# Two of seven additions of exponentials carried out by accumulating transfers from GpSimd's queue

## The chip, the cores and the metric

The kernel runs on one core of one Trainium2 chip. The metric is the time of one execution on the device, in microseconds (us). Before the change three timed runs took 2121.02, 2121.77 and 2122.29 us; their median, 2121.77 us, is the time before. A profile of one further execution is what all readings of the kernel before rest on. TensorE is called PE below, VectorE DVE, ScalarE ACT, GpSimd POOL, and SyncE, which issues nearly all transfers, SP.

## What is computed

Sixteen independent batches of 1024 nodes with 256 channels pass two layers, all in float32. The first layer builds an adjacency weighted by the likeness of node means, makes queries from it, and attends with four heads of 64 channels; the second is two graph convolutions. Each ends in a residual and a layer norm. The part that the change touches is the softmax of the attention:

```
g = relu(einsum('bcn,bnm->bcm', fea, adj * A_s) * para)     # queries, from the weighted adjacency
k, v = split(x @ kv_w)
attn = softmax(einsum('bhnd,bhmd->bhnm', q, k) * scale, axis=-1)
out  = einsum('bhnm,bhmd->bhnd', attn, v)
x = layernorm(x + out)
h = relu(graph_conv(x, adj, w1)); h = relu(graph_conv(h, adj, w2))
x = layernorm(x + (x + h) * 0.5)
```

The softmax is taken without its maximum: the exponentials are summed, and the attention's output is divided by the sum afterwards.

## The kernel before, in words

**Tiles.** A *row tile* is a buffer of 128 partitions by 1024 floats (512 KB in all). There are 31 of them, under one tag, and nearly everything is kept in them: exponentials, sums, weighted adjacency, snapshots, loaded adjacency. A new row tile takes the buffer that has been free the longest by the program's order, and its first writer waits until the last user of that buffer is done. PSUM is cut into three *big* tiles of two banks each (tag `big`) and two tiles of one bank each (tag `bank`).

**Units.** The attention of a batch is done in four units: two pairs of heads (`pair` 0 and 1), and for each pair two halves of 512 queries (`j`). Units 0 and 1 are the first pair, 2 and 3 the second; units 0 and 2 are the first of their pairs. In one unit the 1024 keys are eight tiles of 128 (`mt`, 0 to 7). For each, PE writes the scores of two heads into PSUM (L703), ACT takes the exponential into a row tile `pr` (L710; for `mt` 2 and 6 in two halves from two single banks, L708), and DVE adds the row tiles into a sum `acc`: `pr` 0 plus `pr` 1 (L722), then `pr` 2 to 7 one after the other (L724), seven additions in a unit. Then `turned_sum` transposes the sum in blocks of 32 (L731) and `part_sum` reduces it (L737) to the part of the softmax's denominator.

**Order.** The order of all instructions on each engine is written out by hand: the program is emitted under a manual schedule, every engine and every issuing queue takes its instructions in that order, and one that waits holds up all behind it. The loop over batches overlaps three of them: the attention of batch b, the queries for b+1, the convolutions of b-1 and b-2. From batch 2 on the attention is emitted by `both_units(pair)` (L762): first the scores of the pair's first unit with its additions in between (`collect`, called from `scores` at L713, then `partial` at L715), then the scores of the second unit without additions, then the second unit's additions woven between other steps, the products with the values of the first unit (`outputs`, L749), DVE's transpose of that result out of a big PSUM tile (L774), the products of the second unit into a single bank, and DVE's transpose of that (L778). The single bank that L778 frees is one of the two that the next pair's scores need for the halves of their `mt` 2.

**After the two pairs** PE goes on with the inner product of the first convolution (L903), the joined convolutions (`Joined.run`, L1180 and the products of L1017), the queries of the next batch (L648) and its keys and values. DVE follows with weights (L566, L620 to L623), the division by the denominators (L793 to L799), the sum uT (L1220) with the differences of L1006 to L1008 that the products of L1017 read, and the norms.

**Queues.** SP's queue issues all loads and stores of the steady state, in program order. POOL computes a few sums of the convolution (L1171 to L1174), of the queries (L607 to L610) and the powers for the norms (L361, L316); before the change it issues no transfer.

Batches 0 and 1 have an order of their own; their attention is not touched by the change.

Of the kernel before, what the change touches and what calls it, by code (L numbers as in the profile page):

```python
# [13 lines left out]
ALU = mybir.AluOpType  # L14
# [4 lines left out]
def kernel(  # L19
# [31 lines left out]
    nc = tc.nc  # L51
# [3 lines left out]
    NT = N // P  # L55
# [5 lines left out]
    NJ = N // FB  # L61
# [37 lines left out]
    def row_tile(name):  # L99
        return work.tile([P, N], F32, tag="row", name=name, bufs=ROWS)  # L100
# [16 lines left out]
    for t0 in range(0, NT, 2):  # L117
        nc.sync.dma_start(out=x_first[:, t0:t0 + 2, :],
                          in_=x[0, t0 * P:(t0 + 2) * P, :].rearrange("(t p) c -> p t c", p=P))
# [157 lines left out]
    class NodeSums:  # L277


        def __init__(self, q, xb, name):  # L280
            self.q, self.name = q, name
            self.square = squares[len(taken) % 2]
            taken.append(name)
            q.c_col = self.square[:, 0:NT]
            for t in range(NT):
                nc.scalar.activation(xb[:, t, :], xb[:, t, :], AF.Identity, accum_out=self.square[:, t:t + 1])
# [388 lines left out]
    class Attention:  # L675
# [6 lines left out]
        def __init__(self, b, xB, qT, kT, v):  # L682
            self.b, self.xB, self.qT, self.kT, self.v = b, xB, qT, kT, v
            self.o, self.pr = {}, {}

            self.rden = small.tile([P, len(UNITS) * FB // S], F32, tag="rden", name=f"rden_{b}", bufs=2)
            self.sums = small.tile([P, NC, NB], F32, tag="sums", name=f"sums_{b}", bufs=2)
# [27 lines left out]
                self.partial(u)  # L715

        def collect(self, u, *mts):
            prs = self.pr[u]
            for mt in mts:
                if mt == 1:  # L720
                    self.acc = row_tile(f"acc_{self.b}_{u}")
                    nc.vector.tensor_add(self.acc, prs[0], prs[1])  # L722
                elif mt > 1:
                    nc.vector.tensor_add(self.acc, self.acc, prs[mt])  # L724

        def partial(self, u):
            self.part_sum(u, self.turned_sum(u))
# [863 lines left out]
```

## Time and profile before

The profiled execution took 2121.55 us by its own timing, of which 2119.8 us lie between its first and last instruction (the span). The three timed runs have their median 0.22 us above the profiled one.

| what | value |
|---|---|
| time before, median of 3 runs | 2121.77 us (2121.02 to 2122.29) |
| profiled execution, its own time | 2121.55 us |
| its span | 2119.8 us |
| PE busy | 2108.4 us (99%) |
| DVE busy | 1866.9 us (88%) |
| ACT busy | 1136.1 us (54%) |
| POOL busy | 335.1 us (16%) |
| granted PE clock | 0.999 |
| DMA, moved in all | 346.36 MB, 163 GB/s over the span |
| SP's queue, share of the 16 DMA engines' span | 62.4% |
| one batch in the steady state (start of the scores to the next start) | 130.31 us |

How to read the profile: a busy time is that of one engine, and the engines run beside each other, so that the sum of busy times is no time of the kernel. The page gives busy times by engine, then the chain of work that ended last, followed back from the last instruction, by engine and line, then groups of instructions of one line and form with their count, busy time and mean duration. The timeline lists one engine's instructions in order, merged where several of one line follow each other; in brackets stands the idle time before an instruction and what ended it. A window's row sums what each engine was busy between two times, and the share of the time in which the 16 DMA engines were busy; that share can exceed 1, since the packets of one engine overlap.

### The profile page before, as it was taken

To read this page: it belongs to the slowest core of one execution; us is meant where nothing else is said; L and a number is where in the kernel's file an instruction comes from. 1 tells how busy PE (TensorE), PEld (TensorE's weight loads), DVE (VectorE), ACT (ScalarE), POOL (GpSimd) and SP (SyncE) were. 2 spreads that over 40 slices of the span, in tenths; PEclk is the share of its full clock that TensorE was granted. 3 is DMA by queue.
4 is the path that set the end of the run, shared out by engine and by line. 5 is a ranking of instruction groups with operands and counts; after the bars stand their busy time and mean duration, and the time that the engine had idled before them with its cause. 6 is when DMAs were issued, how large, how long until landed. Compare 5 with 4: busy or idle time off the path is not lost.

```text
span 2119.8 us, 24940 instructions
## 1 busy us (share of the span) xinstructions
PE 2108.4 (99%) x8708; PEld 1031.8 (49%) x8708; DVE 1866.9 (88%) x2271; ACT 1136.1 (54%) x1669; POOL 335.1 (16%) x209
## 2 busy tenths in 40 slices
PE   9999999999999999999999999999999999999998
PEld 5344435445454454545545454454544535445354
DVE  6899998898898988888988889888898888898875
ACT  5745564545646465463654736447355474555523
POOL 2011102131021311203112031210312102131021
PEclk9999999999999999999999999999999999999999
DMA  9495664756639476384864748557495573956545
GB/s 214 121 180 188 131 185 144 153 181 135 204 110 198 175 133 224 104 171 175 142 217 117 160 173 168 196 123 171 150 178 186 142 178 125 191 177 132 176 131 176
DMA packets 613715, 346.36 MB, mean 163 GB/s; under 512 B 491984, under 2 KB 556880, under 8 KB 613584
## 3 DMA queue, kind: packets, MB, share of 16 engines
q1 hardware_dynamic: 613312, 344.45, 62.4%
q8 instruction: 70, 1.15, 0.2%
q14 instruction: 61, 0.50, 0.1%
q10 hardware_dynamic: 272, 0.26, 0.0%
HBM read 294.45 MB, written 50.20 MB: 163 GB/s over the span
## 4 chain that ended last, share of the span: by engine, by line
PE 96%; DVE 1%; SPq 1%; DMA 1%; ACT 0%; issue 0%; POOL 0%; POOLq 0%; DVEq 0%; ACTq 0%
PE s L703 20%; PE av L749 20%; PE hu_ps L1180 17%; PE g_ps L648 16%; PE v_ps L448 4%; PE k_ps L444 4%; PE hu_ps L1017 4%; PE t_ps L903 3%; PE hu_ps L910 2%; PE g_ps L574 1%; PE h_ps L925 1%; PE u_ps L954 1%; PE h_ps L1017 1%; DVE acc L724 1%; SPq L108 1%; SPq L229 0%
## 5 line engine op out<-in xcount | busy, mean ns | idle before, releaser
L724 DVE TENSOR_TENSOR acc<-acc,pr 128x1024 f32<-128x1024 f32 x384 | 481.1, 1253 | 35.0 <-ACT pr L710 0.5
L710 ACT ACTIVATE pr<-s 128x1024 f32<-128x1024 f32 x392 | 391.6, 1120 | 173.0 <-PE s L703 172.7
L703 PE MATMUL s<-qT,kT 64*128 64x512 f32 x2048 | 449.8, 593 | 0.9 <-ACT qT L581 0.6
L749 PE MATMUL av<-pr,v 128*64 128x512 f32 x2048 | 447.0, 594 | 0.0
L703 PEld LDWEIGHTS s<-qT,kT 64*128 64x128 f32 x2048 | 196.5, 187 | 242.6 <-issue 182.2
L749 PEld LDWEIGHTS av<-pr,v 128*64 128x64 f32 x2048 | 144.0, 137 | 297.3 <-issue 270.3
L1180 PE MATMUL hu_ps<-adj,R 128*128 128x512 f32 x480 | 213.6, 592 | 0.0
L361 POOL TENSOR_TENSOR rstd<-rstd,neg_half 128x32 f32<-128x32 f32 x16 | 88.3, 5521 | 624.8 <-DVE rstd L359 624.8
L1171 POOL TENSOR_TENSOR R<-h 128x512 f32<-128x512 f32 x14 | 29.4, 2101 | 811.3 <-DVE o L774 648.7
L566 DVE SCALAR_TENSOR_TENSOR wg<-wg,adj 128x1024 f32<-128x1024 f32 x128 | 150.1, 1211 | 3.6 <-ACT wg L561 3.6
L708 ACT ACTIVATE pr<-s 128x512 f32<-128x512 f32 x240 | 143.1, 708 | 0.7 <-PE s L703 0.7
L560 ACT ACTIVATE wg<-c_row,c_sums 128x1024 f32<-128x1024 f32 x120 | 139.7, 1164 | 2.4 <-DVE wg L566 0.9
L1180 PEld LDWEIGHTS hu_ps<-adj,R 128*128 128x128 f32 x480 | 89.0, 190 | 100.9 <-issue 100.7
L561 ACT ACTIVATE wg<-wg 128x1024 f32<-128x1024 f32 x128 | 135.4, 1057 | 4.1
L906 ACT COPY t<-t_ps 128x1024 f32<-128x1024 f32 x16 | 16.2, 1014 | 175.1 <-PE t_ps L903 175.1
L648 PE MATMUL g_ps<-wg,x 128*128 128x512 f32 x224 | 107.7, 593 | 0.0
L648 PE MATMUL g_ps<-T,xB 128*128 128x512 f32 x208 | 107.3, 597 | 0.0
L648 PE MATMUL g_ps<-wg,xB 128*128 128x512 f32 x208 | 106.2, 592 | 0.0
L1180 PE MATMUL hu_ps<-adj,t 128*128 128x512 f32 x240 | 105.7, 592 | 0.0
L722 DVE TENSOR_TENSOR acc<-pr,pr 128x1024 f32<-128x1024 f32 x64 | 77.8, 1216 | 21.2 <-ACT pr L710 21.1
L731 DVE STREAM_TRANSPOSE accB<-acc 128x1024 f32<-128x1024 f32 x64 | 79.7, 1245 | 2.2
L737 DVE TENSOR_REDUCE den_part<-accB 128x32 f32<-128x1024 f32 x64 | 76.8, 1201 | 1.2
(251 smaller groups left out, 3062.6 us busy)
## 6 DMA issues: line engine op xcount, KB each, us to landing
adj<-adjT SPq DMA_DIRECT2D x210, 512.0 KB
adj<-in_adj_dram SPq DMA_DIRECT2D x128, 512.0 KB
para<-in_L_gnn_para_dram SPq DMA_DIRECT2D x32, 512.0 KB
xB_a<-in_x_dram SPq DMA_DIRECT2D x128, 128.0 KB
x1d<-xB_a SPq DMA_DIRECT2D x128, 128.0 KB
x<-x1d SPq DMA_DIRECT2D x16, 1024.0 KB
xB<-in_x_dram SPq DMA_DIRECT2D x120, 128.0 KB
x<-in_x_dram SPq DMA_DIRECT2D x15, 1024.0 KB
```

Source lines behind the costliest of these rows:

```text
L361: nc.gpsimd.tensor_tensor(self.rstd, self.rstd, neg_half, ALU.pow)
L560: nc.scalar.activation(wg, self.c_row, AF.Abs, bias=self.c_col[:, t:t + 1], scale=-1.0)
L561: nc.scalar.activation(wg, wg, AF.Tanh, scale=-0.5 / C)
L566: nc.vector.scalar_tensor_tensor(wg, wg, 1.0, self.adj.pop(t), op0=ALU.add, op1=ALU.mult)
L648: nc.tensor.matmul(self.p[n], x_n[:, k, :], w_n, start=(k == 0), stop=(k == TJ - 1))
L703: nc.tensor.matmul(halves[s], self.kT[rows, pair, ts(mt, P)], self.qT[rows, pair, ts(j, FB)], start=True, stop=True)
L708: nc.scalar.activation(pr[:, ts(s, FB)], halves[s], AF.Exp)
L710: nc.scalar.activation(pr, ps, AF.Exp)
L724: nc.vector.tensor_add(self.acc, self.acc, prs[mt])
L749: nc.tensor.matmul(pav[s * HD:(s + 1) * HD, :], self.v[:, mt, pair * P + s * HD:pair * P + (s + 1) * HD], prs[mt][:, ts(s, FB)], start=(mt ...
L1017: nc.tensor.matmul(dst[:, ts(t, P)], a[:, ts(t, P)], w, start=first, stop=True, skip_group_check=not first)
L1180: nc.tensor.matmul(dst, self.x[n][:, k, :], of_rows(rows, k), start=(start and k == 0), stop=(k == TJ - 1), skip_group_check=again)
```

## The change

From batch 2 on (14 of 16 batches), the first unit of each pair sums its exponentials in another way. `pr` 0 and 1 are added by DVE into an additional row tile (`acc2`). `pr` 2 and `pr` 3 are added into that tile by two transfers issued from POOL's queue, with addition at the destination. DVE adds `pr` 4 and 5 into `acc`, then `pr` 6 and 7, and last `acc2`. DVE so makes five additions in such a unit and not seven; POOL issues two transfers of 512 KB. There are 28 such units, so 56 transfers. The second unit of a pair and batches 0 and 1 stay as they were.

```diff
         def __init__(self, b, xB, qT, kT, v):
             self.b, self.xB, self.qT, self.kT, self.v = b, xB, qT, kT, v
             self.o, self.pr = {}, {}
+            self.aside = b >= 2
...
         def collect(self, u, *mts):
+            if self.aside and u % NJ == 0:
+                self.collect_aside(u, *mts)
+                return
             prs = self.pr[u]
...
+        def collect_aside(self, u, *mts):
+            prs = self.pr[u]
+            for mt in mts:
+                if mt == 1:
+                    self.aside_acc = row_tile(f"acc2_{self.b}_{u}")
+                    nc.vector.tensor_add(self.aside_acc, prs[0], prs[1])
+                elif mt in (2, 3):
+                    nc.gpsimd.dma_start(out=self.aside_acc, in_=prs[mt], accum_op=ALU.add)
+                elif mt == 5:
+                    self.acc = row_tile(f"acc_{self.b}_{u}")
+                    nc.vector.tensor_add(self.acc, prs[4], prs[5])
+                elif mt > 5:
+                    nc.vector.tensor_add(self.acc, self.acc, prs[mt])
+                if mt == NT - 1:
+                    nc.vector.tensor_add(self.acc, self.acc, self.aside_acc)
```

In the program as built, the second of the two transfers waits on POOL for the first to have landed, since both add into the same tile, and DVE's last addition waits for the second. The additional row tile also moves the buffers of some later row tiles by one place; among them is the first adjacency tile that SP loads for the next batch in the second pair: before, it took the buffer of `accB` of unit 1, and after, that of `acc2` of unit 2.

## The prediction

> **What bounds the kernel now.** I read the page's busy times and chain first, then who waited for whom, then the timeline of one steady batch (913.96 to 1044.27 us; the next starts 130.31 us later).
>
> ```profile
> PE 2108.4 (99%) x8708; PEld 1031.8 (49%) x8708; DVE 1866.9 (88%) x2271; ACT 1136.1 (54%) x1669; POOL 335.1 (16%) x209
> ...
> PE 96%; DVE 1%; SPq 1%; DMA 1%; ACT 0%; issue 0%; POOL 0%; POOLq 0%; DVEq 0%; ACTq 0%
> ```
>
> PE is busy all but 11.4 of 2119.8 us, and the chain that ended last is PE to 96%. The waits of PE itself say the same:
>
> ```profile
> PE idle L1253 <- POOL ident masks.py:199: 1.5, 1, 1.5
> PE good_ps L1534 <- DVE x L1100: 1.0, 1, 1.0
> PE s L703 <- ACT qT L581: 0.6, 1, 0.6
> PE s L703 <- DVE o L778: 0.3, 1, 0.3
> ```
>
> Over the whole run PE waited 1.3 us for DVE. So nothing that DVE saves can shorten the run by more than about that; work taken from DVE is worth nothing unless it comes to stand on PE's path. What DVE can do is be late. The last line names the place: L778 frees the PSUM bank that the next pair's scores need. How late DVE may be is read from its timeline; batch 7, first pair:
>
> ```profile
> 917.11 1.21 DVE L722 TENSOR_TENSOR acc<-pr,pr 128x1024 f32<-128x1024 f32 x1
> 918.43 7.87 DVE L724 TENSOR_TENSOR acc<-acc,pr 128x1024 f32<-128x1024 f32 x6
> 926.33 1.25 DVE L731 STREAM_TRANSPOSE accB<-acc 128x1024 f32<-128x1024 f32 x1
> ...
> 933.23 0.21 DVE L290 STREAM_TRANSPOSE c_turned<-c_sums 128x32 f32<-128x32 f32 x1 [0.60 <-ACT x L286]
> ...
> 941.83 0.72 DVE L778 STREAM_TRANSPOSE o<-av 128x512 f32<-128x512 f32 x1 [1.75 <-PE av L749]
> ```
>
> Between unit 0's sum (done 926.33) and L778 DVE has 0.60 + 1.75 us of idle time. L778 ended at 942.55. PE began the next scores at 941.71 and makes 64 records in 13.93 us, 0.218 each; `mt` 0 and 1 are 8 records, the first half of `mt` 2 another 2, so the second half, which takes L778's bank, begins at 941.71 + 2.18 = 943.89, 1.34 us after L778. Slack of the first pair: 0.60 + 1.75 + 1.34 = 3.7 us. Batches 5, 10 and 14 show the same 0.60 and 1.75.
>
> Second pair: the sum is done at 954.09 (start of L731). Idle behind it: 1.38 us before the L778 at 969.64, then none until uT (L1220, done 996.69). PE reads uT in the products of L1017 some 999.3 (24 records of the third group begin at 1001.12, the two groups before take 0.89 each): 2.65 us later. Slack 1.38 + 2.65 = 4.0 us.
>
> **What the skill says.** "DMA: Bandwidth & Descriptors", *Anatomy of one DMA*: a transfer from GpSimd's queue costs about 2.0 us fixed plus its bytes over 436 GB/s; 512 KB is then 3.2 us, as an estimate. No transfer of that queue is in the trace before, but SP's packets of 4096 bytes took 159 ns at the median, and 8 of them per engine are 1.27 us, which agrees with the 1.20 us of the second term. The same page, *Rules for kernel authors*: an accumulating DMA reads its destination and writes it later, so another access must wait for its semaphore; this is why the second waits for the first. *Queues, rings and completion order*: each DMA engine takes turns between queues packet by packet; no run here shows it yet. "SBUF — State Buffer", *Who interferes with whom*: a DVE addition of two SBUF tiles contends with GpSimd's reads. The trace agrees: L724 took 3.40 us for two at 963.58, beside a POOL addition, against 2.44 for two elsewhere.
>
> **The change part by part.**
>
> *Removed:* two of seven DVE additions in 28 units: 56 x 1.25 us (L724's mean of 1253 ns) = 70 us of DVE's 1866.9. On PE's path: nothing. Even on DVE little comes early: `pr` 5 is only there at 920.74 (ACT's L710), so `pr` 4+5, 6, 7 run from 920.8 at 1.31 us each to 924.7, and the last addition could end at 926.0, 0.3 us before the 926.33 of now.
>
> *Added:* two transfers in a row, and DVE's wait. The first is issued when L722 is done and `pr` 2 is there, 918.4. If one takes T from its issue until the next instruction may go, the last addition starts at the later of 924.7 and 918.4 + 2T and ends 1.3 later. DVE's lateness against now is 918.4 + 2T + 1.3 - 926.33 = 2T - 6.6. Behind the waiting addition on DVE stand L731, L737, the second unit's additions, L774 and L778; who waits for these is PE at the bank. Second pair, same shape: issue 946.1 (L722 at 944.85 plus 1.23), lateness 946.1 + 2T + 1.3 - 954.09 = 2T - 6.7.
>
> *T.* The accumulate reads source and destination, so I double the data term: 2.0 + 2.4 = 4.4 us on idle DMA engines (estimate from the page). Low end 3.2 us, if the second read overlaps. High end about 9, if each packet waits behind a longer turn of SP's. The load differs by pair:
>
> ```profile
> 918.40:925.00 6.60, 6.60 (x34) 2.99 (x32) 6.12 (x5) 6.60 (x10) 0.00 (x0) 1.00 1.04 126
> ...
> 949.00:957.00 8.00, 8.00 (x40) 3.21 (x38) 7.62 (x7) 8.00 (x13) 0.00 (x0) 1.00 0.00 0
> ```
>
> The last two columns are the DMA share and GB/s: in the first pair SP's short packets fill the engines (1.04), in the second they are idle. An even share of the engines doubles the data term once more, 2.0 + 4.8 = 6.8; with turns by packet the long packets get more than half. First pair: between 4.4 and 6.8, I take 6.1. Second pair: 4.5.
>
> *Sum.* First pair: lateness 2 x 6.1 - 6.6 = 5.6, less the 3.7 of slack: PE waits 1.9 us. Second: 2 x 4.5 - 6.7 = 2.3, within its 4.0: nothing. A stall of PE shifts everything behind it alike, so it is not given back: 14 x 1.9 = 27 us. Against the profiled execution's own time 2121.55 + 27 = 2148.2; the median lies 0.2 above that: 2148.
>
> *Costed at nothing, with the cover.* POOL: after the two issues it has nothing until L1171 at 963.68, and L1172 waits until 974.56 anyway; a second pair of transfers later than that would delay the convolution. SP: the first adjacency load of the next batch (943.67) now waits for the last addition of unit 2, to about 957; the load behind it already waits for unit 2's L737 and goes at 956.61, and the reader is L566 at 971.38, so 10 us cover it. SP's own transfers lose 29 MB worth of engine time beside 346, in stretches whose loads are read 15 us or more later. ACT: its `wg` tile takes the buffer of `acc` of unit 2, so L560 at 957.55 may wait some 2 us; ACT then idles 9 us before L906. Descriptor writing may slow a DVE addition by up to 1 us: inside T's range.
>
> **Rivals.**
>
> *Hidden after all* (26%). If 2T stays under 10.3 in the first pair (T about 5.1) the slack takes all, and the time is that of before, 2121.8. For it: 4.4 us is the page's own price, and SP's packets there are 128 bytes, so they yield fast. Against it: both transfers lie wholly in stretches with shares of 1.04 to 0.88.
>
> *The turns are long* (20%). If a turn of SP's is many of its short packets, or the addition itself is slow, T is some 9 in the first pair and 6.5 in the second: lateness 11.4 and 6.3, waits of 7.7 and 2.3, 14 x 10 = 140 us: 2262. For it: 475,616 packets of 128 bytes in SP's queue. Against it: they take 13 ns each.
>
> *Faster* (2%): needs PE idle time to give back; the ends of the run hold at most the 1.3 us above, under a tenth of a per cent. That the change moves no work is excluded: DVE makes two additions fewer in each unit as built.
>
> **The numbers.** Forecast 52% (T of 5.2 to 7.5 in the first pair; 2123 to 2190), hidden 26%, long turns 20%, faster 2%. A measurement tells about 0.2%, 4 us, from no change. Faster 0.02, same 0.26, slower 0.72. The range takes in the hidden case and half of the long turns: 2120 to 2215.
>
> **What would show it.** DVE's busy time falls to about 1797 us. DVE's last addition has an idle time before it of about 6 us in the first pair and 2.5 in the second, put down to the transfer. PE's L703 waits for L778 about 1.9 us per batch, 27 in all, and for nothing else new; the batch takes 132.2 us. I am wrong if PE waits elsewhere (L1017 for uT, L648 for weights), if the second pair waits as long as the first, or if the batch stays at 130.31.

## The result, and the profile after

The changed kernel takes 2202.24 us (median of 4 runs, 2196.49 to 2206.62) against 2121.72 us before (4 runs, 2121.02 to 2122.29): a ratio of 1.038, 95% interval 1.035 to 1.041. That is 80 us slower, where the forecast was 27. The profiled execution is the shortest of the four, 2196.49 us with a span of 2194.7 us, 74.9 us above the span before; the granted PE clock is 0.990 where it was 0.999.

From the page of the kernel after, the busy times, three groups (the last two columns are busy time and mean, then the idle time before and who ended it), and the issue line of the new transfers (median us from issue to landing last):

```profile
PE 2137.8 (97%) x8708; PEld 1050.8 (48%) x8708; DVE 1784.5 (81%) x2215; ACT 1140.9 (52%) x1669; POOL 385.5 (18%) x265
...
L704 PE MATMUL s<-qT,kT 64*128 64x512 f32 x2048 | 478.6, 610 | 45.6 <-DVE o L798 45.6
...
L744 DVE TENSOR_TENSOR acc<-acc,acc 128x1024 f32<-128x1024 f32 x28 | 34.3, 1225 | 157.0 <-DMA acc<-pr 157.0
...
acc<-pr POOLq DMA_DIRECT2D x56, 512.0 KB, 5.3
```

DVE does 56 instructions less, 82 us of work, and it waits 157 us for the transfers. PE, whose instructions are the same 8708, is busy 29 us longer than before, and waits 46 us more. Its waits name the place (L798 is the L778 of before, L704 the L703; the lines behind the new function have moved by 20):

```profile
PE s L704 <- DVE o L798: 45.6, 14, 10.8
PE idle L1273 <- POOL ident masks.py:199: 1.5, 1, 1.5
PE good_ps L1554 <- DVE x L1120: 1.0, 1, 1.0
```

Fourteen waits, one in each of batches 2 to 15, all where the prediction put them: the scores of the second pair wait for the bank that DVE's last copy out of the first pair frees. The second pair makes none. Batch 7 on DVE, first pair (start, duration, what; in brackets the idle time before it):

```profile
952.37 1.22 DVE L735 TENSOR_TENSOR acc<-pr,pr 128x1024 f32<-128x1024 f32 x1
...
957.35 2.56 DVE L742 TENSOR_TENSOR acc<-acc,pr 128x1024 f32<-128x1024 f32 x2
968.31 1.23 DVE L744 TENSOR_TENSOR acc<-acc,acc 128x1024 f32<-128x1024 f32 x1 [8.40 <-DMA acc<-pr]
969.57 1.25 DVE L751 STREAM_TRANSPOSE accB<-acc 128x1024 f32<-128x1024 f32 x1
...
982.58 0.67 DVE L798 STREAM_TRANSPOSE o<-av 128x512 f32<-128x512 f32 x1
```

and on POOL, both pairs:

```profile
954.12 0.92 POOL L737 DMA_DIRECT2D acc<-pr  x1 [14.31 <-DVE acc L735]
961.36 0.86 POOL L737 DMA_DIRECT2D acc<-pr  x1 [6.33 <-DMA acc<-pr]
986.30 0.86 POOL L737 DMA_DIRECT2D acc<-pr  x1 [24.08 <-ACT pr L709]
991.99 0.86 POOL L737 DMA_DIRECT2D acc<-pr  x1 [4.82 <-ACT pr L711]
```

PE begins batch 7 35.25 us later than before, because of the batches ahead, and DVE's first addition moves with it (917.11 before). The sum's transpose begins at 969.57, where 926.33 + 35.25 = 961.58 would be on time: DVE is 8.0 us late. The two transfers take 954.12 to 968.31, 14.2 us or 7.1 each. Over the 14 batches this stretch has a mean of 13.6 us (11.9 to 16.6); in the second pair it is about 10.2.

**Where the 74.9 us are.** Three terms, read on PE in batches 7 and 9, second pair:

```profile
976.96 2.84 PE L704 MATMUL s<-qT,kT 64*128 64x512 f32 x10
983.30 13.94 PE L704 MATMUL s<-qT,kT 64*128 64x512 f32 x54 [3.50 <-DVE o L798]
...
1248.99 2.84 PE L704 MATMUL s<-qT,kT 64*128 64x512 f32 x10
1253.50 12.28 PE L704 MATMUL s<-qT,kT 64*128 64x512 f32 x54 [1.67 <-DVE o L798]
```

Undisturbed, the 64 records show as one line of 14.00 us. Batch 9 takes 1248.99 to 1265.78, 16.79 us; less its idle time of 1.67 that is 15.12, still 1.12 more than 14.00. The products of the two halves normally run side by side (their records start at the same moment); those on either side of the wait run alone, so that ten records take 2.84 us and not 10 x 0.218 = 2.18, and the drain of the last one, which shows as busy, stands open too. That is 1.12 us for each wait, whatever its length. The Trainium skill, "TensorE: Matmul & The Clock Gate", *Part 3: Packing small matmuls — row/col tiling*, says that products in distinct row groups of the array run concurrently; the trace agrees, and shows what it costs when one has to come alone.

Batch 7 takes 20.28 us: less 3.50 of idle time and the 15.12 there remain 1.66. The windows of the two, from the first product behind the wait (columns: stretch, length, busy PE, PEld, DVE, ACT, POOL with records, granted clock, DMA share, GB/s), say what it is:

```profile
983.30:986.70 3.40, 3.40 (x8) 1.52 (x10) 2.18 (x2) 0.60 (x1) 0.40 (x1) 0.50 1.02 380
1253.50:1256.90 3.40, 3.40 (x16) 1.66 (x18) 2.18 (x2) 1.98 (x3) 0.68 (x1) 1.00 1.02 387
```

Behind the wait of batch 7 the granted clock is half for 3.4 us, and 8 records of PE fall into it where batch 9 has 16. Eight of the 14 waits are followed by such a stretch: seven of 3.41 us, each costing about 1.7, and one of 13.65 us in batch 2. The same page, *Part 1: The HAM clock gate (the "warmup" mystery)*, says that the clock falls to 4/8 after an idle window of 3413 ns, counted by windows that run freely. The 0.50 and the 3.41 us agree; but here a wait of 2.3 us was enough in batch 4 and one of 3.1 was not in batch 12, so it is not a whole idle window that decides.

The traces show more when time is cut by these windows. All lowered stretches of this run begin whole multiples of 3.413 us from each other, to within 0.003 us. Continued to either side, this grid gives two windows for batch 4 (its wait is over at 576.05) and two for batch 12 (over at 1653.89):

```profile
573.66:577.07 3.41, 1.13 (x7) 0.55 (x8) 3.38 (x5) 0.88 (x2) 0.00 (x0) 1.00 0.96 293
577.07:580.48 3.41, 3.41 (x12) 1.39 (x10) 1.16 (x2) 1.62 (x2) 0.86 (x1) 0.50 1.02 392
...
1648.87:1652.28 3.41, 1.88 (x8) 0.57 (x4) 3.34 (x5) 2.43 (x3) 0.00 (x0) 1.00 0.72 179
1652.28:1655.69 3.41, 1.80 (x8) 0.88 (x10) 3.41 (x4) 0.60 (x1) 0.00 (x0) 1.00 0.98 384
```

The shorter wait lies within one window, which PE so spends idle for 2.28 us, and the next window is at half clock. The longer one is split, 1.53 and 1.61 us, and no window is lowered. In batches 2 to 15 of this run and of a1, c2, d1, d2 and d3 below, every full-clock window with 2.07 us or more of idle PE was followed by half clock, and none with up to 1.96 us was. In other runs less was enough: 1.93 us in d4 (between other products), 1.85 us in b2 and 1.44 in b3, so that about 2 us is no fixed limit.

One wait is 10.8 us, in batch 2. Here is batch 2 before, and the same line after:

```profile
288.72 2.84 PE L703 MATMUL s<-qT,kT 64*128 64x512 f32 x10
291.88 12.28 PE L703 MATMUL s<-qT,kT 64*128 64x512 f32 x54 [0.32 <-DVE o L778]
```

```profile
302.03 14.94 PE L704 MATMUL s<-qT,kT 64*128 64x512 f32 x54 [10.77 <-DVE o L798]
```

This is the wait of 0.3 us that the prediction quoted from before: in batch 2 DVE was already the late one, so its slack there was nothing, and the whole of the new lateness shows.

The sum: 45.6 - 0.3 of idle time, 13 x 1.12 = 14.6 for the waits that are new, 14.5 of lower clock (7 x 1.70, 2.66 in batch 2) = 74.4 of the 74.9 us. The 29 us that PE is busy longer are the last two of these terms.

### The profile page after: what moved, and what is told of

It is laid out like the page before. It is cut to its first block, busy times and chain, and to the rows that moved or that the text cites. A ratio compares the mean times of both kernels' runs of the same rounds, so it can differ in the third digit from the quotient of the medians.

```text
span 2194.7 us, 25011 instructions
## 1 busy us (share of the span) xinstructions
PE 2137.8 (97%) x8708; PEld 1050.8 (48%) x8708; DVE 1784.5 (81%) x2215; ACT 1140.9 (52%) x1669; POOL 385.5 (18%) x265
## 5 line engine op out<-in xcount | busy, mean ns | idle before, releaser
L704 PE MATMUL s<-qT,kT 64*128 64x512 f32 x2048 | 478.6, 610 | 45.6 <-DVE o L798 45.6
L704 PEld LDWEIGHTS s<-qT,kT 64*128 64x128 f32 x2048 | 214.8, 192 | 297.8 <-issue 189.1
L728 DVE TENSOR_TENSOR acc<-acc,pr 128x1024 f32<-128x1024 f32 x216 | 273.2, 1265 | 16.8 <-ACT pr L711 0.5
L737 POOL DMA_DIRECT2D acc<-pr x56 | 49.2, 878 | 672.4 <-DVE acc L735 347.1
L744 DVE TENSOR_TENSOR acc<-acc,acc 128x1024 f32<-128x1024 f32 x28 | 34.3, 1225 | 157.0 <-DMA acc<-pr 157.0
L740 DVE TENSOR_TENSOR acc<-pr,pr 128x1024 f32<-128x1024 f32 x28 | 34.3, 1225 | 84.0 <-ACT pr L711 84.0
```

The costliest lines, as they stand in the source:

```text
L704: nc.tensor.matmul(halves[s], self.kT[rows, pair, ts(mt, P)], self.qT[rows, pair, ts(j, FB)], start=True, stop=True)
```

## The experiments

Theory: all of the loss is the first pair's DVE lateness above its slack, with what a wait of PE brings along. Rivals: the second pair has a share; the transfers slow others by their traffic; the additional tile and its buffers do it.

**One pair only.** The condition `u % NJ == 0` becomes:

```diff
-            if self.aside and u % NJ == 0:
+            if self.aside and u == 0:      # a1_first_pair
+            if self.aside and u == NJ:     # a2_second_pair
```

> The transfers only in the first pair of each batch (unit 0), the second pair as before the change. Theory (two transfers in a row end too late for DVE's last addition, which holds up the transpose that frees PE's bank; only the first pair has too little slack): nearly the whole loss stays, 2190 to 2207 us, with some 45 us of PE waiting for L798. Rival (the cost is the 56 transfers' traffic, or comes from both pairs alike): half of the loss, near 2160 us.

> The transfers only in the second pair (unit 2), the first pair as before the change. Theory: the second pair's lateness of about 4 us is within its slack of 4.0, so 2121 to 2127 us and no wait of PE for DVE. Rival (both pairs alike): near 2160 us.

First pair alone: 2200.89 us, ratio 1.038 (1.036 to 1.040). Second pair alone: 2124.81, ratio 1.0016 (1.0009 to 1.0023). The waits of PE, first of a1, then of a2:

```profile
PE s L704 <- DVE o L798: 45.6, 14, 11.1
```

```profile
PE hu_ps L1037 <- DVE uT L1240: 3.2, 5, 0.6
```

The first pair is the whole loss. The second stands at the edge of its slack: five waits at the product that the prediction had named (L1017 of before), 3 us in all. In a2 the sum of unit 2 is 3.2 to 5.8 us late, and the five batches that wait are those with more than 4.4. With both pairs changed even these waits are absent: there PE itself comes out of the second pair's scores later, by 6.28 us in batch 7, and against that DVE is at most 3.8 us late in any batch.

**Traffic without the wait; the wait's removal without traffic.** In a3 DVE makes all seven additions, and the same 56 transfers go into a tile that nobody reads. In a4 DVE makes the five additions and no transfer is issued, so that exponentials 2 and 3 are missing from the sums.

```diff
             if self.aside and u % NJ == 0:
                 self.collect_aside(u, *mts)
-                return
...
-                    nc.vector.tensor_add(self.aside_acc, prs[0], prs[1])
+                    nc.gpsimd.memset(self.aside_acc, 0.0)
...
-                elif mt == 5:
...
-                if mt == NT - 1:
-                    nc.vector.tensor_add(self.acc, self.acc, self.aside_acc)
```

```diff
-                elif mt in (2, 3):
-                    nc.gpsimd.dma_start(out=self.aside_acc, in_=prs[mt], accum_op=ALU.add)
```

> DVE makes all seven additions as before the change; the same 56 transfers are issued at the same places, but add into a tile that POOL has filled with zeros and that nobody reads. Only the traffic, the issuing and the additional row tile are left. Theory (the wait is the cost): 2121 to 2125 us. Rival (traffic, descriptor writing or moved buffers cost): 2140 us or more.

> The five additions of the changed kernel without the transfers, so exponentials 2 and 3 are missing from the sums of the first units from batch 2 on. Theory: PE is the bound and 70 us less on DVE bring nothing, 2120.5 to 2122.5 us. Rival (DVE held PE somewhere that the waits do not show): some us faster, below 2117 us.

a3: 2122.31 us, ratio 1.0005 (0.9996 to 1.0014). a4: 2119.94, ratio 0.9994 (0.9985 to 1.0003), half a microsecond below the range I had expected. The traffic, POOL's issues and the tile cost nothing that can be told from noise (0.14% at most by the interval), and DVE's additions in a3 are not slowed by the issuing beside them (1867.2 us busy, before 1866.9). DVE's saving brings at most the 1.3 us by which a4 lies under the median of before, in which the wait of batch 2 is gone. What is left as the cost is that DVE waits.

**The wait moved behind other work.** b1 issues the same transfers, but the last addition of the first unit stands behind all of the second unit's additions, where the transfers have landed. With it go the transpose and the reduction of that sum, and the second unit's own transpose stands behind the copy that frees the bank, which takes 1.25 us of work from in front of the copy.

```diff
-            if summed:
+            if summed and not (self.aside and u % NJ == 0):
                 self.partial(u)
...
-                if mt == NT - 1:
-                    nc.vector.tensor_add(self.acc, self.acc, self.aside_acc)
...
+            first_acc, aside_acc = self.acc, self.aside_acc
...
-            accB = self.turned_sum(u + 1)
+            second_acc = self.acc
+            nc.vector.tensor_add(first_acc, first_acc, aside_acc)
+            self.acc = first_acc
+            self.partial(u)
...
-            self.part_sum(u + 1, accB)
+            self.acc = second_acc
+            self.partial(u + 1)
```

> All 56 transfers and five additions as in the changed kernel, but the first unit's last addition, its transpose and its reduction stand on DVE behind the second unit's additions, and the second unit's transpose and reduction behind L798's transpose. Theory (what costs is the place of the wait, ahead of the transpose that frees the bank): the transfers have landed by then, no wait of PE, 2121 to 2125 us. Rival (the chain of two transfers costs wherever its result is taken): 2140 us or more.

Measured 2121.78, ratio 1.0002 (0.9993 to 1.001): the loss is gone with all 56 transfers in place. DVE in batch 7; the last addition shows no idle time before it, as in 27 of the 28 units (1.4 us in the other):

```profile
938.17 1.22 DVE L796 TENSOR_TENSOR acc<-acc,acc 128x1024 f32<-128x1024 f32 x1
...
941.84 0.70 DVE L800 STREAM_TRANSPOSE o<-av 128x512 f32<-128x512 f32 x1
```

The copy that frees the bank starts at 941.84, as in the kernel before (941.83). DVE's busy share is 84%, 4 points below before, and the time is the same: PE bounds.

**Shorter chains of transfers.** b2 gives the two transfers a tile each (2 into 0+1, 5 into 3+4), so that they need not follow each other. b3 makes one transfer and six DVE additions.

```diff
-                elif mt in (2, 3):
-                    nc.gpsimd.dma_start(out=self.aside_acc, in_=prs[mt], accum_op=ALU.add)
+                elif mt == 2:
+                    nc.gpsimd.dma_start(out=self.aside_acc, in_=prs[2], accum_op=ALU.add)
+                elif mt == 4:
+                    self.aside_acc2 = row_tile(f"acc3_{self.b}_{u}")
+                    nc.vector.tensor_add(self.aside_acc2, prs[3], prs[4])
...
+                    nc.gpsimd.dma_start(out=self.aside_acc2, in_=prs[5], accum_op=ALU.add)
...
+                    nc.vector.tensor_add(self.acc, prs[6], prs[7])
                     nc.vector.tensor_add(self.acc, self.acc, self.aside_acc)
+                    nc.vector.tensor_add(self.acc, self.acc, self.aside_acc2)
```

```diff
-                elif mt in (2, 3):
+                elif mt == 2:
...
-                elif mt == 5:
+                elif mt == 4:
...
-                    nc.vector.tensor_add(self.acc, prs[4], prs[5])
+                    nc.vector.tensor_add(self.acc, prs[3], prs[4])
-                elif mt > 5:
+                elif mt > 4:
```

> Two transfers and five additions per first unit, but into two tiles: exponential 2 into the sum of 0 and 1, exponential 5 into the sum of 3 and 4; neither waits for the other. Theory (two landings in a row make the 14 us of the first pair): the second lands some 11 us after the first is issued and not 14, lateness near 3.5 us against a slack of 3.7, so 2121 to 2135 us, with waits left in the first batches. Rival (one loaded transfer alone is too slow): 2160 us or more.

> Only exponential 2 is added by a transfer; DVE makes six additions. Theory: one transfer of about 7 us lands when DVE reaches its last addition, lateness under 1.5 us in most batches, 2121 to 2124 us. Rival (one loaded transfer alone is too slow): 2150 us or more.

b3: 2123.49, ratio 1.0009 (1.0003 to 1.0016), with one wait, 1.4 us, in batch 2. b2: 2156.96, ratio 1.017 (1.015 to 1.019), between what the theory (2121 to 2135) and the rival (2160 or more) had led me to expect. Its waits:

```profile
PE s L704 <- DVE o L801: 15.1, 11, 5.8
```

In batch 7 its second transfer is issued 2.8 us after the first (938.52 and 935.76), because it needs DVE's addition of 3 and 4, and lands some 7.5 us later beside SP's loads: DVE is 4.2 us late there, beyond the slack. From the first issue to DVE's last addition these two take 10.4 us, where two in a row took 14.2: shorter, not half.

**Is it the clock?** b4 and c1 repeat the product ahead of the waiting one, to keep PE at work while it waits (5 and 3 times in place of one).

```diff
-                    nc.tensor.matmul(halves[s], self.kT[rows, pair, ts(mt, P)], self.qT[rows, pair, ts(j, FB)],
-                                     start=True, stop=True)
+                    again = 4 if self.aside and (u, mt, s) == (NJ, 2, 0) else 0
+                    for _ in range(1 + again):
+                        nc.tensor.matmul(halves[s], self.kT[rows, pair, ts(mt, P)], self.qT[rows, pair, ts(j, FB)],
+                                         start=True, stop=True)
```

> The changed kernel, with the score product just ahead of the waiting one (first half of key tile 2 of unit 2) made five times in place of once, so that PE works through part of the wait. Theory (27 of the 80 us are no waiting but a lower PE clock after it, drain and refill included, and the clock falls because PE stood idle): the waits that are left are too short for the clock to fall, except in batch 2; 2178 to 2192 us, mean clock about 0.996. Rival (the clock falls for another reason, or the wait alone makes the loss): the redundant products only take the wait's place, 2195 us or more.

> As b4, but the product ahead of the waiting one is made three times in place of once: two more, which b4's profile shows to take 0.86 us each when no partner runs beside them, 1.7 us, less than the shortest wait of the changed kernel counted from start to start (1.8 us). So the redundant work lies inside the waits, and any difference to the changed kernel is the clock's. Theory (the clock falls after idle PE and costs some 17 us of the 80): 2184 to 2194 us. Rival (the clock's fall does not come from the idle time): 2197 to 2207 us as the changed kernel.

b4: 2192.84 (2187.47 to 2195.02), ratio 1.033. c1: 2194.32 (2192.31 to 2197.37), ratio 1.034. Both stand just outside what I expected, and both are inconclusive: a repeat takes 0.86 us when alone, so that b4's four are 3.4 us per batch and as long as most waits themselves, and in c1 the clock still fell six times, two of them behind waits of only 1.45 and 1.61 us. The clock term rests on the windows above and on d1 and d2 below, not on these.

**What makes the transfers long.** On quiet DMA engines the first packet comes 1.43 us after the issue, 128 packets of 4096 bytes (340 ns each, where SP's copies of that size take 159) fill 2.8 us, and POOL's next issue follows the last packet by 0.9: 5.1 us. DVE goes sooner, 0.4 us after the last packet: 4.6 us. In the first pair a transfer took 4.6 to 10.8 us, 6.7 in the mean of batches 3 to 15. c2 turns SP's 128-byte packets in that stretch into 4096-byte ones; c3 is the kernel before with the same edit.

```diff
-                for a in range(Q):
-                    c0 = cc * P + a * S
-                    nc.sync.dma_start(out=nodes[:, c0:c0 + S].rearrange("(bn k) r -> k bn r", k=S),
-                                      in_=by_node(self.xB[cc][a * S:(a + 1) * S, :]))
+                nc.sync.dma_start(out=nodes[ts(cc, FB), :].rearrange("(p t) c -> p (t c)", p=P), in_=self.xB[cc])
...
-                    coming = load_x(b + 2, str(b + 2)), load_blocked(b + 2, str(b + 2))
+                    coming = load_x(b + 2, str(b + 2)), load_plain(b + 2, str(b + 2))
```

> The changed kernel, with the loads of the next batch's blocked input and the stores of the normed nodes made in plain rows of 4096 bytes in place of 128-byte pieces: the same bytes in far fewer packets, in the stretch of the first pair's transfers. It changes which node and channel a value stands for, and so what is computed, not how much. Theory (the first pair's transfers are slower than the second's because SP's queue keeps the DMA engines full there): they take some 10.5 us for two in place of 13.6, the lateness of 4 to 5 us nearly fits the slack, 2122 to 2145 us. Rival (the first pair's transfers are slow for another reason): 2185 us or more.

> The kernel before the change with the same plain rows, as the measure for c2; it too changes what is computed. Both theories: PE is the bound, 2119 to 2123 us.

c3: 2122.56, ratio 1.0008 (0.9999 to 1.0017), so the edit itself is neutral. c2: 2182.88, ratio 1.028 (1.027 to 1.030), where I had expected 2122 to 2145. With the short packets gone the second transfer runs as on quiet engines, 4.6 us in batch 7. But two loads, of 512 KB and 1 MB, that SP had queued behind the short packets came earlier, and the first transfer met those. In batch 7 it was issued at 941.61, its packets ran from 944.89 to 949.11, and the next could go only after 8.4 us. So it is not the short packets as such that hold a transfer up. d4 moves these loads behind the first pair as well.

```diff
-            if c2:
+            if c2 and not more:
...
-                    c2.load_x()
...
+                    c2.load_h1()
+                    c2.load_x()
```

> As c2 (plain rows; what is computed is changed in the same way), and besides the loads of the first convolution's hidden values and of the stored nodes, which in c2 stood in SP's queue just ahead of the first transfer, are issued behind the first pair. Theory (the first pair's transfers wait for what SP has queued): both take about 5.1 us there, lateness 4 to 4.5 us, 14 x 1 us lost: 2127 to 2145 us. Rival (another cause): 2175 us or more as c2.

d4: 2167.14, ratio 1.022 (1.020 to 1.023), where I had expected 2127 to 2145. What it shows is on POOL, batch 7 (two issues of the first pair, two of the second), and in PE's waits:

```profile
938.08 0.92 POOL L734 DMA_DIRECT2D acc<-pr  x1 [14.19 <-ACT pr L708]
944.26 0.86 POOL L734 DMA_DIRECT2D acc<-pr  x1 [5.27 <-ACT pr L706]
966.55 0.86 POOL L734 DMA_DIRECT2D acc<-pr  x1 [21.43 <-ACT pr L706]
976.94 0.86 POOL L734 DMA_DIRECT2D acc<-pr  x1 [9.52 <-ACT pr L706]
```

```profile
PE hu_ps L1034 <- DVE uT L1237: 19.9, 12, 1.9
```

The first pair is now quiet: from its first issue to the last addition 10.8 us. (The release named before the second and the fourth issue is ACT's, which had long been done; what ended these two waits was the landing.) But the loads, which SP now issues at 959 us with four adjacency loads behind them, are in flight when the second pair's transfer is issued at 966.55. Its first packet comes at 970.70, 4.2 us after the issue, in which the engines' share is 1.05, and the next transfer can go only after 10.4. The second pair, harmless until then, now stalls PE at uT, twelve times, 19.9 of the 46 us lost; I did not add up the rest. The cost follows what SP has queued to wherever it stands: this part of the theory is confirmed, by a run that missed its number.

**The lateness by itself.** What was still open was whether lateness of this size, with no transfer at all, gives the whole loss. The kernel before gets additional, unused DVE additions behind the first unit, six in d1, four in d2, three in d3:

```diff
+            if pair == 0:
+                spare = row_tile(f"spare_{self.b}")
+                for _ in range(6):
+                    nc.vector.tensor_add(spare, self.pr[u][6], self.pr[u][7])
```

> The kernel before the change, all seven additions on DVE and no transfer; in batches 2 to 15, after the first pair's first unit, DVE makes six redundant additions into a spare row tile, 6 x 1.28 = 7.7 us of lateness, about that of the changed kernel in most batches (8.0 in batch 7). Theory (DVE's lateness beyond 3.4 us is the whole loss, and the clock follows from PE's idle time): 14 x 4.3 = 60 us and some 15 to 24 for the clock, 2190 to 2206 us, mean clock 0.99. Rival (the transfers' traffic or POOL adds to it, or lowers the clock): below 2185 us, with the clock near 0.999.

> As d1 with four redundant additions, 5.1 us of lateness. Theory: 14 x 1.7 = 24 us, of which most waits leave PE idle under 1 us, so that the clock falls seldom; 2143 to 2156 us. Rival (any wait lowers the clock): 2165 us or more.

> As d1 with three redundant additions, 3.8 us of lateness. Theory (slack 3.4 us): 14 x 0.4 = 6 us, 2125 to 2131 us. Rival (slack 3.7 us, as predicted): 2121 to 2124 us.

How late DVE is can be read in batch 7 between two starts, the transpose of the first unit's sum (L731) and the second unit's first addition (L722): 2.42 us before, and 6.07, 7.33 and 9.85 in d3, d2 and d1.

| run | DVE late by | time, us | ratio (interval) | PE idle at the bank | clock |
|---|---|---|---|---|---|
| d3 | 3.65 us | 2131.02 | 1.005 (1.003 to 1.007) | 4.0 | 0.998 |
| d2 | 4.91 us | 2149.73 | 1.013 (1.012 to 1.015) | 11.9 | 0.997 |
| d1 | 7.43 us | 2201.74 | 1.038 (1.036 to 1.040) | 47.1 | 0.989 |

```profile
959.71 7.52 DVE L770 TENSOR_TENSOR spare<-pr,pr 128x1024 f32<-128x1024 f32 x6
...
977.73 0.68 DVE L782 STREAM_TRANSPOSE o<-av 128x512 f32<-128x512 f32 x1
```

```profile
PE s L703 <- DVE o L782: 47.1, 14, 7.8
```

d1 and d2 are within what I expected, d3 at its upper edge. d1 is the changed kernel's time without one transfer, at a like lateness (the changed kernel's is 7.1 us in the mean of batches 3 to 15, and 10.5 in batch 2).

The three also give the slack. The second pair's scores of batch 7, before and in d3:

```profile
941.71 14.00 PE L703 MATMUL s<-qT,kT 64*128 64x512 f32 x64
...
947.72 14.29 PE L703 MATMUL s<-qT,kT 64*128 64x512 f32 x64
```

Of d3's 3.65 us most batches lose 0.29, of d2's 4.91 most lose 1.12 + 0.44 of idle time, and of d1's 7.43 most lose 1.12 + 2.95. Each time 3.36 us are swallowed. And they separate the clock: from d2 to d1 the lateness grows by 2.5 us, 14 x 2.5 = 35 us, the time by 52. The other 17 are the clock, which fell behind 11 of d1's 14 waits and in d2 behind batch 2's long one alone, none of the 13 short ones: ten stretches more, 10 x 1.7 = 17.

## Why the prediction was right and wrong

*Right: the mechanism and the place.* PE bounds, DVE's saving brings nothing (a4), DVE waits for two transfers in a row, and that delays L778's copy and PE's scores. The runs show it: a1, a2, b1, d1. That the second pair costs nothing was right by less than forecast: lateness was to be 2.3 us against a slack of 4.0, and alone (a2) it is 3.2 to 5.8 and makes PE wait five times. In the changed kernel PE's own delay covers it, which the prediction did not have: this part was right in part by luck.

*The step that failed is the sum*, "PE waits 1.9 us ... 14 x 1.9 = 27 us". Its terms, against what was measured:

- *2T in the first pair:* 12.2 forecast; 13.4 in the mean of batches 3 to 15, 6.7 a transfer. What was too low is the price on quiet engines: 2 x 4.4 = 8.8 forecast, 5.1 + 4.6 = 9.7 measured. (The 4.4 was an estimate, the page's fit with its data term doubled.) What the load adds was about right, 3.4 forecast and 3.6 measured: the first packet comes after 2.05 us in the mean and not 1.43, and the packets take 3.96 us and not 2.77. Single transfers differ much more, 4.6 to 10.8 us. The turns by packet that the Trainium skill tells of ("DMA: Bandwidth & Descriptors", *Queues, rings and completion order*) do not show at a transfer's start: up to 5.0 us pass there before its first packet (batch 3). +1.2 us.
- *The issue:* taken at the end of L722's counterpart; POOL goes 0.53 us after it or a little later (0.63 in batch 2). +0.5 us.
- *The slack:* 3.7 forecast, 3.4 measured (d1 to d3). I let the waiting half begin after the first half's products, at 943.89; in the trace before they start together, at 943.53. +0.3 us.
- *Batch 2:* the 0.3 us wait of before was quoted and passed over. It meant a slack of nothing there, so that this batch alone pays its whole lateness, 10.5 us. That is 6.6 more than a usual one: 3.4 for the slack, and 3.2 because its two transfers took 16.6 us.
- *The clock:* the sum has no term for it; it takes a wait of PE to cost its own length. In eight batches PE came back at half clock. 14.5 us.

From forecast to measurement: 1.9 + 1.2 + 0.5 + 0.3 = 3.9 us in 13 batches (measured: 34.8 of idle time and 14.6 of broken pairs, 49.4 / 13 = 3.8), 10.5 in batch 2, 14.5 of clock: 13 x 3.8 + 10.5 + 14.5 = 74.4 us.

The weakness was in the shape of the sum: a wait is what is left of two numbers near each other, 5.6 of lateness and 3.7 of slack. Two microseconds on these, a seventh of the stretch they come from, doubled the wait.

*The rivals.* Hidden after all: would have needed 2T under 10.3, with the measured issue and slack under 9.5; the first pair's shortest is 11.9. Long turns: a T of 9 in the mean of two was not reached (8.3 at most, batch 2), though single transfers took 9.1 and 10.8. *The signs:* DVE's busy time was to be 1797 and is 1784.5 (a4, the same instructions without transfers, has 1800.1; the rest I did not follow up). Idle time before the last addition was to be about 6 and 2.5; it is 6.0 to 9.6 in the first pair of batches 3 to 15, and 1.6 to 4.4 in the second pair. The batch was to be 132.2 and is 135.2 in the mean of batches 3 to 14.

*What stays open.* Why a transfer's first packet comes after 1.78 us in batch 7, where the DMA share meanwhile is 1.41, and after 5.03 us in batch 3, where it is 0.88, is not shown; the load alone does not tell it. How much idle time in a window lowers the clock is known only for the waits of these runs. The changed kernel's runs spread by 10 us, where those of before spread by 1.3. Their granted clock is 0.990, 0.989, 0.988 and 0.988 in the order of their times; 0.002 of 2200 us are some 4 us (an estimate), so the clock is a part of the spread. The rest is open, since only one of these runs left a trace.

No version here beats the kernel before. b1 equals it with DVE less loaded.

## What to carry to other kernels

Where the bound engine is PE, price a waiting step on another engine by lateness less slack, batch by batch, and take a small wait that the profile already shows as a batch without slack. A PE wait costs more than its idle time: in this kernel 1.12 us around it came on top and, where some 2 us of it fell into one window of the clock's grid, a stretch at half clock. Where a transfer replaces an addition, place its consumer far behind it on the waiting engine, as b1 does; here that gave the whole loss back, and none of the attempts at shorter or quieter pairs of transfers (b2, c2, d4) did.

## What the runs showed of the hardware that was not expected

- An accumulating transfer of 512 KB between SBUF tiles takes 5.1 us from issue to the next issue on quiet engines, its 4096-byte packets 340 ns against 159 for SP's copies; in the first pair, beside SP's traffic, it took 4.6 to 10.8.
- A wait between two 64-row products costs 1.12 us beyond the idle time that the profile shows.
- Waits of 0.4 to 0.8 us never lowered PE's clock (13 in d2); those of 2.95 to 3.3 us did so 10 times in 13 (d1), each time for 3.41 us, which costs 1.7.
- The lowered stretches of a run begin on one grid of 3.413 us; where a wait lies on it decided, beside its length, whether the clock fell.
